# Five written instruction orders of a graph network's third layer, rewritten

## The chip, the cores and the metric

The kernel runs on one core of one Trainium2 chip. The metric is the device time of one execution in microseconds. The times shown are the median of three runs, with the lowest and highest, and beside them stands one more execution, which the hardware profiler recorded.

## The reference, cut to what matters

128 graphs of 64 nodes with 256 features pass through four layers. Each layer adds its result to its input and normalizes each node's 256 features.

```python
x = _layernorm(x + L0(x, adj, ...))   # five groups of 25 nodes, two graph convolutions each
x = _layernorm(x + L1(x, adj, W, b))  # one graph convolution
x = _layernorm(x + L2(x, adj, ...))   # a polynomial of the normalized adjacency, leaky relu
x = _layernorm(x + L3(x, adj, ...))   # five rounds of a gated recurrent unit:
# A = (adj != 0); h = x
# for l in range(5):
#     m = h @ weight[l];  agg = A^T m per graph
#     r, z = sigmoid(...); n = tanh(i_n + r * h_n);  h = (1 - z) * n + z * h
# x = _layernorm(x + h)
```

The reference numbers its layers from 0. All data are float32.

## The kernel before

The 128 graphs lie in 16 chunks of 8. Layer 0 comes first (up to about 320 us of the span). Layer 3 fills the rest, and layers 1 and 2 of the later chunks are done inside it.

**Steps of layer 3.** A step s (there are 79 in the loop) is one of the five rounds of one chunk. Two chunks alternate: step s works on chunk x, while w is the chunk of the step before, whose gates are being finished. Ten steps are a cycle: five rounds of an even chunk and five of an odd one, one after the other. Within a step the instructions stand in a written order, a string of names in `ORDERS` (L67). Sequence "p" serves steps 2 to 7 of a cycle; "8", "9", "0" and "1" serve the other four. `step` (L1138) walks through the string and issues what each name stands for. The loop runs under a manual schedule, so every engine (TensorE, VectorE, ScalarE, GpSimd and SyncE's DMA queue) executes its own share in exactly the order of the string. There is no planner at run time: an engine waits at the head of its queue until the data are there.

The names in the strings:

- R1 to R7 and N1 to N7: the seven products of a Strassen-like scheme on TensorE (L837), for the gates r and z together (eight 128x256 matmuls each) and for n (four each). Products 1, 6, 7 and 4 add into one PSUM bank a, in that order of use. Product 2 has bank b; 5 and 3 share bank d.
- r1, r6, r7 and n1, n6, n7: ScalarE copies the running content of bank a (L857), before the next product adds to it.
- A2, A7, A3 and B2, B7, B3: VectorE adds a copy to bank b or d (L861).
- S: two sigmoids on ScalarE (L938). X, x: the reset gate, two VectorE instructions (L995, L996). T, t: tanh (L953). U, u: the update, three VectorE instructions (L958 to L960). Capital letters belong to the step's own chunk, small ones to w. The digit (2, 7, 4 or 3) is the quarter of the state.
- f0, f1: VectorE transposes half of w's new state and SyncE writes it to DRAM (L974, L980). d0, d1: SyncE fetches it back, transposed (L988). G: the next round's messages: sixteen 128x128 matmuls on TensorE (L254), two ScalarE copies (L256), and three GpSimd sums Ta (L817 to L819).
- e, h: three GpSimd sums Th of the new state. y: two VectorE transposes and DMAs for the chunk that comes next. l: loads of the adjacency and x of a later chunk.
- p: one piece of other work: `output` of a finished chunk (L1074, four pieces), or else one piece of `mid` (L265), layers 1 and 2 of a coming chunk (19 pieces for each of two chunks in a cycle).

In `mid` the pieces that matter here are: the statistics of layer 1's result (L359), the pass that normalizes it (L362; four VectorE instructions of L185, one for each pair of graphs), the gather that multiplies the normalized rows with the polynomial (L366; TensorE again at L254, `pa<-poly,xt`), and at the end of layer 2 the statistics and the second normalizing pass (L381, L384). In the steady cycles, for the first chunk of a pair, L362 is the fifth p of step 3, L366 is the first p of step 4, and L384 is the first p of step 5. For the second chunk L362 is the fourth p of step 7, L366 the fifth p of step 7, and L384 the fifth p of step 8.

After the loop a short end runs the last round of the last chunk. It takes only the order of x, t and u from sequence "9" (L1211).

Of the kernel before, what the change touches and what calls it, by code (L numbers as in the profile page):

```python
# [41 lines left out]
class Unit:  # L42
# [23 lines left out]

ORDERS = {  # L67
    "p": """
u3 u4 R1 r1 t7 p R2 u7 l R5 h f0 f1 e R6 r6 d0 N1 A2 n1 N2 B2 p S2 N6 R7 X2 r7
n6 T2 p N5 R4 y A7 U2 N7 S7 n7 p S4 R3 B7 A3 N4 S3 X7 d1 N3 B3 X3 X4 G p T4 T3  # L70
""",
    "8": """
u4 l R1 R5 R2 t7 u3 f0 u7 e r1 R6 f1 N1 h p n1 p N2 d1 A2 r6 B2 N6 S2 d0 R7 N5
r7 X2 p n6 A7 R4 N7 p y n7 R3 B7 S4 S7 N4 A3 T2 X7 X4 N3 S3 B3 X3 U2 p T4 G T3
""",
    "9": """
u4 t7 l R1 R5 p R2 r1 u7 A2 u3 f0 h d0 R6 f1 p r6 p N1 d1 n1 N2 S2 B2 X2 R7 N6
r7 N5 n6 T2 N7 A7 U2 y R4 n7 R3 p S4 S7 e B7 N4 A3 S3 G N3 p X7 X4 B3 X3 p T4
T3
""",  # L80
    "0": """
l u4 t7 u3 R1 u7 R5 f0 R2 r1 R6 f1 N1 A2 h n1 r6 N2 S2 N6 R7 n6 B2 y N5 r7 p X2
N7 d0 T2 A7 n7 p B7 p e d1 U2 S7 R4 R3 A3 G S4 N4 p S3 N3 B3 X4 X3 T4 X7 T3
""",
    "1": """
u4 p t7 u3 f0 R1 R2 u7 R5 h l r1 f1 R6 r6 N1 N2 e n1 A2 N6 d0 R7 S2 B2 n6 r7 N5
p A7 N7 X2 n7 d1 T2 y p R4 B7 p R3 S7 A3 U2 S4 N3 B3 N4 S3 G X7 X3 X4 T4 T3 p
""",
}

# [1200 lines left out]
```

## Time and profile before

| what | value |
|---|---|
| median of three runs | 2134.34 us (2134.17 to 2135.53) |
| the profiled execution's own time | 2135.55 us |
| its span, first to last instruction | 2133.7 us |
| TensorE busy | 2109.1 us, 99% |
| VectorE busy | 1641.0 us, 77% |
| ScalarE busy | 979.1 us, 46% |
| GpSimd busy | 592.6 us, 28% |
| granted TensorE clock, mean | 0.997 |

"Busy" means that at least one instruction is in flight. TensorE's matmuls overlap, so a small wait between two of them can vanish in the busy share. In an undisturbed run of 128x256 matmuls one starts every 216 ns although each is recorded as 379 ns long; of 128x128 matmuls one starts every 111 ns. Waits are therefore best read from the starts. VectorE and GpSimd both work in SBUF, and how long a VectorE instruction takes here depends on what GpSimd does at the same time.

### The profile page before, as it was taken

What the parts mean: (1) busy time and instruction counts of PE and PEld (TensorE: products, weight loads), DVE (VectorE), ACT (ScalarE), POOL (GpSimd) and SP (SyncE); (2) the same over time, 40 slices, a digit from 0 to 9 for tenths busy, and PEclk for the clock granted to TensorE, in tenths of its full rate; (3) what the DMA queues carried; (4) which work ended last, traced back from release to release, by engine and by line L of the source; (5) the groups of instructions that cost most, each with busy time, mean ns of one, the idle gap of its engine ahead of it and who ended that gap; (6) DMA issues with size and microseconds to landing.
All of it is one profiled execution on the core that took longest, in us unless ns stands there. A gap on an engine that the chain in (4) does not pass through costs nothing.

```text
span 2133.7 us, 31438 instructions
## 1 busy us (share of the span) xinstructions
PE 2109.1 (99%) x10738; PEld 1819.5 (85%) x10738; DVE 1641.0 (77%) x3849; ACT 979.1 (46%) x2006; POOL 592.6 (28%) x638
## 2 busy tenths in 40 slices
PE   9999999999999999999999999999999999999997
PEld 6777788888888888888888888888888888888886
DVE  3345566787988798788878898879887987888776
ACT  3333334444544454444544454544444554445443
POOL 3411121222332233222323232223222232223321
PEclk9999999999999999999999999999999999999998
DMA  6642110223421342124322342124212421233221
GB/s 167 178 133 62 36 41 21 55 60 75 90 65 40 73 91 75 47 59 78 86 50 50 70 95 68 47 65 93 71 40 65 96 68 46 55 69 91 50 50 40
DMA packets 522059, 149.80 MB, mean 70 GB/s; under 512 B 488734, under 2 KB 516924, under 8 KB 521900
## 3 DMA queue, kind: packets, MB, share of 16 engines
q1 hardware_dynamic: 516996, 142.58, 27.7%
q0 software_dynamic: 2192, 4.80, 0.9%
q8 instruction: 85, 1.39, 0.3%
q10 hardware_dynamic: 2712, 0.42, 0.1%
q14 instruction: 74, 0.61, 0.1%
HBM read 82.70 MB, written 65.01 MB: 69 GB/s over the span
## 4 chain that ended last, share of the span: by engine, by line
PE 91%; DVE 6%; DMA 1%; issue 1%; POOL 0%; ACT 0%; SPq 0%; POOLq 0%; DVEq 0%; ACTq 0%
PE parz L837 24%; PE pdrz L837 12%; PE pan L837 12%; PE pa L254 9%; PE pbrz L837 6%; PE pdn L837 6%; PE pd L333 5%; PE ps L524 5%; PE ph L508 4%; PE pbn L837 3%; PE pa L492 1%; PE pp L314 1%; PE po L546 1%; DVE xt L185 1%; PE pf L644 1%; DVE NI L996 1%
## 5 line engine op out<-in xcount | busy, mean ns | idle before, releaser
L857 ACT COPY c<-parz 128x512 f32<-128x512 f32 x240 | 140.0, 583 | 369.8 <-PE parz L837 368.8
L837 PE MATMUL parz<-Th,WHH 128*128 128x256 f32 x960 | 289.0, 383 | 2.9 <-ACT c L857 2.9
L938 ACT ACTIVATE RZ<-RZ,brz 128x256 f32<-128x256 f32 x474 | 214.9, 503 | 166.8 <-DVE RZ L861 166.7
L817 POOL TENSOR_TENSOR Ta<-agg 128x512 f32<-128x512 f32 x80 | 102.7, 1284 | 660.0 <-ACT agg L256 660.0
L837 PE MATMUL parz<-Ta,V 128*128 128x256 f32 x960 | 286.0, 380 | 0.0
L837 PEld LDWEIGHTS parz<-Th,WHH 128*128 128x128 f32 x960 | 178.9, 190 | 35.6 <-ACT c L857 10.4
L837 PEld LDWEIGHTS parz<-Ta,V 128*128 128x128 f32 x960 | 182.5, 190 | 24.8
L953 ACT ACTIVATE NI<-NI,bih 128x256 f32<-128x256 f32 x316 | 152.6, 506 | 109.2 <-DVE NI L996 108.9
L857 ACT COPY c<-pan 128x512 f32<-128x512 f32 x237 | 138.4, 584 | 130.4 <-PE pan L837 130.2
L170 POOL TENSOR_TENSOR rs<-ve,mhalf 128x4 f32<-128x4 f32 (+2 forms) x65 | 66.7, 1027 | 393.3 <-DVE ve L163 340.8
L959 DVE TENSOR_TENSOR RZ<-RZ 128x256 f32<-128x256 f32 x316 | 161.1, 510 | 10.8
L817 POOL TENSOR_TENSOR Th<-hn 128x512 f32<-128x512 f32 x64 | 81.5, 1274 | 293.1 <-DVE hn L960 281.3
L861 DVE TENSOR_TENSOR NI<-pdn,c 128x512 f32<-128x512 f32 x158 | 108.2, 685 | 59.9 <-ACT c L857 44.9
L861 DVE TENSOR_TENSOR RZ<-pdrz,c 128x512 f32<-128x512 f32 x160 | 109.7, 686 | 46.4 <-PE pdrz L837 25.3
L837 PE MATMUL pan<-Ta,V 128*128 128x256 f32 x474 | 145.4, 388 | 0.0
L995 DVE SCALAR_TENSOR_TENSOR NI<-NI,bhh,RZ 128x256 f32<-128x256 f32 x237 | 119.7, 505 | 30.2 <-ACT RZ L938 21.3
L837 PE MATMUL pan<-Th,WHH 128*128 128x256 f32 x474 | 141.0, 379 | 0.0
L958 DVE TENSOR_TENSOR RZ<-hn,NI 128x256 f32<-128x256 f32 x252 | 115.6, 459 | 27.8 <-ACT NI L953 27.2
L254 PEld LDWEIGHTS pa<-A,h 128*128 128x128 f32 x1024 | 124.4, 192 | 3.3
L254 PE MATMUL pa<-A,h 128*128 128x128 f32 x1024 | 124.6, 275 | 0.0
L256 ACT COPY agg<-pa 128x512 f32<-128x512 f32 x160 | 92.9, 583 | 62.9 <-PE pa L254 62.4
L960 DVE TENSOR_TENSOR hn<-RZ,NI 128x256 f32<-128x256 f32 x256 | 113.7, 444 | 9.1
(228 smaller groups left out, 4739.7 us busy)
## 6 DMA issues: line engine op xcount, KB each, us to landing
hb<-flip SPq DMA_DIRECT2D x184, 256.0 KB
h<-hb SPq DMA_DIRECT2D x624, 64.0 KB
out_dram<-xt SPq DMA_DIRECT2D x30, 256.0 KB
hT<-hb SPq DMA_DIRECT2D x112, 64.0 KB
W<-in_w_dram SPq DMA_DIRECT2D x10, 512.0 KB
xt<-xb SPq DMA_DIRECT2D x32, 156.0 KB
xo<-in_x_dram SPq DMA_DIRECT2D x9, 512.0 KB
xb<-xo SPq DMA_DIRECT2D x9, 512.0 KB
```

Source lines behind the costliest of these rows:

```text
L254: nc.tensor.matmul(p[:, q * 128 : (q + 1) * 128], src(q, k), m[:, q, :], start=True, stop=True)
L333: nc.tensor.matmul(p[:, h, :], ag[:, k, q * 128 : (q + 1) * 128], W[:, k, :], start=k == 0, stop=k == 1)
L817: nc.gpsimd.tensor_sub(t[:, 0:2, :], a[:, :, H:], a[:, 0, :].rearrange("p (s n) -> p s n", s=2))
L837: nc.tensor.matmul(bank[:, g, :], w[:, q, i - 1, :], rhs, start=i in (1, 2, 5) and g == 0 and m == 0, stop=m == len(side) - 1, skip_group_ ...
L857: nc.scalar.copy(c, self.a)
L861: nc.vector.tensor_add(v, self.b if i == 2 else self.d, self.copies.pop({7: 7, 2: 1, 3: 6}[i]))
L938: nc.scalar.activation(v, self.g.a[:, q, :] if i == 4 else v, AF.Sigmoid, bias=brz[:, 2 * q + j : 2 * q + j + 1])
L953: nc.scalar.activation(n, n, AF.Tanh, bias=bih[:, 4 + j : 5 + j])
L958: nc.vector.tensor_sub(d, self.hT[:, j, f], n)
L959: nc.vector.tensor_mul(d, d, z)
L960: nc.vector.tensor_add(self.hn[:, j, f], d, n)
L995: nc.vector.scalar_tensor_tensor(n[:, j, f], h, bhh[:, 4 + j : 5 + j], r[:, j, f], op0=ALU.add, op1=ALU.mult)
```

## The change

All five strings are replaced; nothing else is touched. Each new string holds the same names, so the same instructions are issued. Sequence 8 has one p more and sequence 9 one fewer (those had nothing to issue in the steady cycles), and in the steady cycles every piece stays in its step.

```diff
     "p": """
-u3 u4 R1 r1 t7 p R2 u7 l R5 h f0 f1 e R6 r6 d0 N1 A2 n1 N2 B2 p S2 N6 R7 X2 r7
-n6 T2 p N5 R4 y A7 U2 N7 S7 n7 p S4 R3 B7 A3 N4 S3 X7 d1 N3 B3 X3 X4 G p T4 T3
+t7 h u4 R1 u3 p l R2 u7 R5 r1 f0 f1 R6 d0 N1 r6 N2 n1 A2 e S2 B2 p R7 X2 N6 r7
+n6 T2 p A7 N5 R4 N7 S7 U2 n7 S4 p R3 N4 B7 A3 N3 S3 X7 d1 X4 B3 G p X3 T4 T3 y
 """,
     "8": """
-u4 l R1 R5 R2 t7 u3 f0 u7 e r1 R6 f1 N1 h p n1 p N2 d1 A2 r6 B2 N6 S2 d0 R7 N5
-r7 X2 p n6 A7 R4 N7 p y n7 R3 B7 S4 S7 N4 A3 T2 X7 X4 N3 S3 B3 X3 U2 p T4 G T3
+u4 t7 u3 R1 R5 p l f0 p u7 f1 h R2 d0 r1 R6 N1 n1 d1 N2 N6 p A2 r6 n6 S2 B2 y
+e R7 X2 N5 r7 A7 R4 N7 p n7 B7 S4 R3 N4 p S7 A3 X4 N3 B3 X7 S3 G X3 T2 p T3 U2
+T4
 """,
     "9": """
-u4 t7 l R1 R5 p R2 r1 u7 A2 u3 f0 h d0 R6 f1 p r6 p N1 d1 n1 N2 S2 B2 X2 R7 N6
-r7 N5 n6 T2 N7 A7 U2 y R4 n7 R3 p S4 S7 e B7 N4 A3 S3 G N3 p X7 X4 B3 X3 p T4
-T3
+t7 h R1 u4 R5 u3 r1 R2 A2 p u7 f0 R6 r6 d0 f1 N1 n1 N2 S2 l R7 r7 N6 n6 N5 B2 X2
+N7 A7 p d1 T2 R4 R3 p U2 S7 n7 e S4 y A3 B7 N4 S3 G N3 p X7 B3 X3 X4 T3 T4 p
 """,
     "0": """
-l u4 t7 u3 R1 u7 R5 f0 R2 r1 R6 f1 N1 A2 h n1 r6 N2 S2 N6 R7 n6 B2 y N5 r7 p X2
-N7 d0 T2 A7 n7 p B7 p e d1 U2 S7 R4 R3 A3 G S4 N4 p S3 N3 B3 X4 X3 T4 X7 T3
+t7 u4 h u3 u7 R1 R5 R2 r1 R6 f0 r6 f1 e N1 n1 A2 S2 N2 R7 N6 r7 n6 l B2 p N5 X2
+A7 N7 T2 d0 n7 R4 d1 p R3 B7 p S7 G S4 p A3 U2 N3 N4 B3 S3 X4 y X3 T3 X7 T4
 """,
     "1": """
-u4 p t7 u3 f0 R1 R2 u7 R5 h l r1 f1 R6 r6 N1 N2 e n1 A2 N6 d0 R7 S2 B2 n6 r7 N5
-p A7 N7 X2 n7 d1 T2 y p R4 B7 p R3 S7 A3 U2 S4 N3 B3 N4 S3 G X7 X3 X4 T4 T3 p
+p t7 R1 u7 u4 f0 u3 d0 R2 r1 R5 e A2 f1 R6 N1 n1 N2 r6 N6 n6 B2 p R7 S2 N5 r7 h
+l N7 n7 X2 y A7 T2 R4 R3 d1 p B7 p A3 U2 S7 N4 N3 S4 S3 B3 X4 G X3 T4 X7 T3 p
 """,
```

Read engine by engine, most names keep their neighbours. What moves is this:

- TensorE, sequence p: R7 and N6 change places. Sequence 8: the two products of layer 2 (p, p) stand before R2 instead of after N1. Sequence 0: R7 and N6 as well as N3 and N4 change places; sequence 1: N3 and N4. Sequence 9: no change.
- VectorE, sequence p: X4 moves ahead of B3, and X3 moves from ahead of the fifth p to behind it; u3 and u4 change places. Sequence 8: the second normalizing pass moves from the end (behind X3 and U2) to a place between B7 and A3; y moves ahead of X2; X7 moves behind B3. Sequences 9, 0 and 1: updates and gates change places among themselves; in sequence 1 X2 goes ahead of A7.
- ScalarE, sequence p: r1 moves from ahead of t7 to behind the first p; S2 moves ahead of the second p and S4 ahead of the fourth. Sequence 8: r1 stands behind the four evictions of the two products.
- GpSimd: the same order. SyncE: d0 before d1 in sequence 8; y's DMAs earlier in sequence 8; in sequence 1, d0's fetches stand ahead of f1's write; in sequence 0, the first output's stores stand behind d1.

## Prediction

> **What bounds the kernel now.** I read the page first: its busy line and the chain that ended last.
>
> ```profile
> span 2133.7 us, 31438 instructions
> ...
> PE 2109.1 (99%) x10738; PEld 1819.5 (85%) x10738; DVE 1641.0 (77%) x3849; ACT 979.1 (46%) x2006; POOL 592.6 (28%) x638
> ...
> PE 91%; DVE 6%; DMA 1%; issue 1%; POOL 0%; ACT 0%; SPq 0%; POOLq 0%; DVEq 0%; ACTq 0%
> ```
>
> TensorE carries the chain, and no edit removes a matmul. A new order can only win what TensorE waits. The busy share hides that, since overlapped matmuls look busy while they wait. So I read the starts in the timeline: 216 ns is the undisturbed step of a 128x256 matmul, 111 ns of a 128x128. The excess over these, summed over the starts, is 4.36 us in a steady cycle of ten steps (227.4 us; mean of the six cycles from step 10 to 69). By step: 0: 0.33, 1: 0.09, 2: 0.16, 3: 0.07, **4: 1.99**, 5: 0.61, 6: 0.09, 7: 0.16, 8: 0.33, 9: 0.52. The first ten steps wait 2.1 us together, the last nine of the loop 2.0. All of layer 3's loop therefore holds about 26 + 4 = 30 us, or 1.4%, and no order can give more.
>
> Who ends these waits, from the waits view (us in total, times, longest):
>
> ```profile
> PEld pa L254 <- DVE xt L185: 11.2, 18, 0.8
> PE pa L254 <- DVE xt L185: 6.4, 18, 0.4
> PEld pan L837 <- ACT c L857: 10.7, 46, 0.3
> PEld parz L837 <- ACT c L857: 10.4, 40, 0.9
> PEld pdrz L837 <- DVE RZ L861: 4.6, 12, 0.6
> ```
>
> The first two lines are one place, 3 matmuls in each of 6 cycles: the gather at the start of step 4 waits for the pass of L362. The timeline of one such place (start, length, instruction):
>
> ```profile
> 1318.42 0.68 DVE L861 TENSOR_TENSOR NI<-pdn,c 128x512 f32<-128x512 f32 x1
> 1319.20 0.48 DVE L995 SCALAR_TENSOR_TENSOR NI<-NI,bhh,RZ 128x256 f32<-128x256 f32 x1
> ...
> 1320.58 0.42 DVE L996 TENSOR_TENSOR NI<-pan,NI 128x256 f32<-128x256 f32 x1
> 1320.76 1.27 POOL L817 TENSOR_TENSOR Ta<-agg 128x512 f32<-128x512 f32 x1 [3.21 <-ACT agg L256]
> ...
> 1320.92 3.19 DVE L185 TENSOR_SCALAR xt<-xt,mv,rs 128x256 f32<-128x256 f32 x4
> ...
> 1322.23 0.49 PE L254 MATMUL pa<-poly,xt 128*128 128x128 f32 x2 [0.45 <-DVE xt L185]
> ...
> 1323.04 0.49 PE L254 MATMUL pa<-poly,xt 128*128 128x128 f32 x2 [0.32 <-DVE xt L185]
> ...
> 1323.84 1.70 PE L254 MATMUL pa<-poly,xt 128*128 128x128 f32 x12 [0.32 <-DVE xt L185]
> ```
>
> The pass starts 0.16 us after GpSimd's sums Ta (2.9 us for three), and each of its instructions ends just after one of the sums. Its four take 3.19 us; outside sums, in step 37, four take 1.37. The gather's first matmul was due at 1321.62 (R1 at 1319.89 plus eight times 0.216).
>
> **What the Trainium skill says.** "SBUF — State Buffer", section "Who interferes with whom": VectorE and GpSimd share one port pair, taken as an exclusive lock for a whole instruction; tensor_scalar in a two-port mode and any VectorE instruction with two SBUF inputs contend, one with an input in PSUM does not. The trace agrees: L185 406 ns free, 880 to 1256 under a sum; L959 425 against 990 on average; L861, which reads PSUM, 685 against 676. The pages put no price on the waits of this change; all durations below are the trace's.
>
> **The change part by part.** No instruction is added or removed. GpSimd's order is the same, so the sums stay where their inputs put them. On SyncE the loads l stay ahead of f0, and in sequence 0 an output's two stores go behind d1's fetches: nobody waits for a store.
>
> (a) *First pass, sequence p.* In step 43 VectorE had A3 to 1317.65, X7 to 1318.50, B3, X3, X4 to 1321.00, the pass to 1324.11. In the new order X4 follows X7: its product N4 ends at 1317.41 and its sigmoid S4 at 1316.24, so it runs 1318.42 to 1319.35; B3 (N3 ends 1318.27) to 1319.95; the pass starts at 1319.9, one microsecond earlier. One starts every 0.32 us, so three are through or in flight when Ta comes at 1320.76, and the fourth waits for one sum (1.28) and ends near 1322.35. The gather reads it at 1321.62 + 6 x 0.111 = 1322.29. The wait shrinks from 1.98 to about 0.2 us (0 to 0.8): **-1.78 a cycle**.
>
> (b) *What goes under the sum instead.* X3 (0.93 us, both inputs in SBUF) follows the pass. Under the sums I estimate it at 1.3 to 1.9. T3 waits for X3; behind T3 on ScalarE stand t7 and now r1 (0.5 + 0.5 + 0.6 us), and R6 waits for r1. Laid out from the trace: after step 3, X3 ends near 1323.9, r1 near 1326.5 (behind the gather's two copies), R6 is due at 1326.86: covered by 0.3. After steps 2, 5 and 6 the cover is 0.6, 0.7 and 2 us. After step 4 there is no TensorE piece between R1 and R6: statistics to 1349.3, X3 to 1350.2-1351.3, r1 to 1351.9-1352.95, R6 due at 1352.21. I take 0.3 (0 to 0.75). Step 5's waits at R3 and N3 (0.44) come from a late VectorE, which now starts u4 0.3 earlier; I keep 0.1. Net -0.04.
>
> (c) *R7 ahead of N6.* N6 waits for n1, copied while only N2 runs (0.08 in steps 2 and 5, 0.06 in 6); R7 fills that gap. R4 waited for r7 behind N5 alone (0.08 in 5 and 7); now N6 stands between too. R7's own copy r6 ends at R6 + 0.7, with N1 and N2 (1.73) as cover. **-0.38**.
>
> (d) *Sequence 8.* R7's wait of 0.24 for r6 goes (r6 ends 0.4 before R7). But r1 now stands behind four evictions of layer 2's products and ends at about R6's due time: +0.2; N6 behind N2 alone: +0.08. The second pass runs off the sums (1.4 us instead of 1.8) but waits for its GpSimd root, about 1.1 us after the statistics; behind it A3, S3 and X3, whose product N3 ends later anyway. y comes 5.7 us earlier: its two transposes (0.69 each) fill VectorE's wait for the sigmoid S2 ahead of X2, and its ten DMAs stand on SyncE behind d0 and d1 as before, with nothing of this step after them: free. Net +0.03.
>
> (e) *Sequences 9, 0, 1.* VectorE leaves step 8 about 1.4 us earlier, so R3's wait in 9 goes: -0.11; R5's 0.26 for Ta stays, its order is the same. In 0, N6's 0.13 goes, but T4 and t7 come later behind X3, X4: R6 and R3 +0.2; net +0.07. In 1, A7 now waits for X2 (0.93), and ends where R3 is due: +0.2 (0 to 0.5). In 1, d0's fetches precede f1's write, but f0's write lands (2.57 us) before f1 is transposed: free, with 1.4 us to spare before G; if that cover goes, G waits by what is missing.
>
> Sum: -1.78 - 0.04 - 0.38 + 0.03 - 0.11 + 0.07 + 0.2 = **-2.0 a cycle**, -12.1 in six. First ten steps: -0.6 by (c). Last nine: no pieces, (c) alone, six times 0.16: -1.0. The end, where R6 waits 2.3 us for a copy behind T3: T3 comes earlier, the updates not; I take -1 (-3.8 to +2, unknown). Together **-14.7 us**. Against the profiled execution's own 2135.55 (span 2133.7 and 1.85 around it) that is 2120.9; the median of the runs shown lies 1.2 lower, so **2119.6**.
>
> VectorE doesn't become the bound: 190.3 us busy in a cycle of 227.4.
>
> **Rivals.** *The likeliest (0.76)*, as above. Its own range is 2112 (no residual waits, the end at its best) to 2129.
>
> *The pass stays under the sum (0.10).* If S4 or N4 holds X4 up, or the sums take the lock before the second instruction of the pass, (a) falls to about -0.2: -14.7 + 6 x 1.6 = -5, so 2129 to 2131. For it: only 0.86 us separate pass and sum. Against: both of X4's inputs are ready a microsecond before.
>
> *Slower: the gate X3 takes the pass's place under the sum (0.11).* In all steps 2 to 7 of a cycle r1 now hangs on X3, T3 and t7. It decides when R6 waits more than 14.7/36 = 0.41 us a step on average. At 0.7 us, which needs X3 some 1.0 us later than I lay it out in most steps, the cost is 36 x 0.7 = 25, the net +10.5, and the time 2145. Against: four of the six places have 0.6 us of cover or more.
>
> *Small mishaps cancel the gain (0.03)*: 2134.
>
> **How the numbers follow.** This kernel's runs can tell about 0.2%, 4.3 us, from no change. Faster by more: the likeliest case, and half of the one where the pass stays under: 0.80. Within: 0.09. Slower: the gate case: 0.11. The range 2111 to 2134 holds the likeliest and the pass rival with their bounds and leaves the slower one out.
>
> **What would show it.** In step 4 the gather's matmuls follow R1 at 111 ns with at most the fourth pair late, and L185's mean in xt falls from 521 ns; the two lines of L254 on L185 in the waits shrink to under 3 us. Steps 2 to 7 lose their 0.08s at N6 and R4. New lines, if I am wrong: parz on c L857 growing beyond 10 us with R6 of steps 3 to 8 as the waiter, and pdrz on RZ L861 in step 1. A steady cycle above 227 us refutes the sum.

## The result and the profile after

| | before | after |
|---|---|---|
| median of six runs each | 2134.82 us (2133.23 to 2135.56) | 2124.94 us (2124.42 to 2125.68) |
| profiled execution: span | 2133.7 us | 2123.7 us |
| TensorE busy | 2109.1 us | 2102.9 us |
| VectorE busy | 1641.0 us | 1661.1 us |

The changed kernel takes 0.9954 of the time before (95% interval 0.9943 to 0.9964): 9.9 us less. The forecast of 2119.6 us is 5.3 us too low; its sum was -14.7.

The page after, busy line and chain:

```profile
span 2123.7 us, 31527 instructions
...
PE 2102.9 (99%) x10738; PEld 1820.6 (86%) x10738; DVE 1661.1 (78%) x3849; ACT 978.9 (46%) x2006; POOL 594.8 (28%) x638
...
PE 86%; DVE 10%; issue 1%; DMA 1%; ACT 0%; SPq 0%; POOL 0%; DVEq 0%; POOLq 0%; ACTq 0%
```

TensorE still carries the chain. VectorE is busy 20 us longer with the same 3849 instructions: something else now lies beside GpSimd's sums.

Where the 9.9 us lie, from the starts of R1 in both traces: first ten steps 223.59 to 223.00 us, the six cycles 1365.95 to 1359.23, steps 70 to 77 of the last nine 160.93 to 159.88, the rest from step 78 on 57.30 to 55.78. That is -0.6, **-6.7**, -1.05 and -1.5; the prediction had -0.6, **-12.1**, -1.0 and -1. Almost the whole error lies in the steady cycles.

There, the excess of the starts of TensorE's matmuls over their undisturbed steps, in us for a cycle, by step (the measure of the prediction; in all kernels against the undisturbed steps of the kernel before):

| step | 0 | 1 | 2 | 3 | 4 | 5 | 6 | 7 | 8 | 9 | sum |
|---|---|---|---|---|---|---|---|---|---|---|---|
| before | 0.33 | 0.09 | 0.16 | 0.07 | 1.99 | 0.61 | 0.09 | 0.16 | 0.33 | 0.52 | 4.36 |
| after | 0.44 | 0.41 | 0.53 | 0.07 | 0.09 | 0.79 | 0.09 | 0.08 | 0.47 | 0.28 | 3.24 |
| predicted change | +0.07 | +0.2 | -0.08 | 0 | -1.78 | -0.20 | -0.06 | -0.08 | +0.03 | -0.11 | -2.0 |
| measured change | +0.11 | +0.32 | +0.37 | 0 | -1.90 | +0.18 | 0 | -0.08 | +0.14 | -0.24 | -1.1 |

Step 4 did what was said. In the waits view of after (total us, times, longest) the two lines of L254 on L185 are gone; the waits for the copies c (r and n) became fewer, and the longest of them longer:

```profile
PEld parz L837 <- ACT c L857: 12.5, 27, 1.9
PEld pan L837 <- ACT c L857: 8.3, 31, 0.6
```

The timeline of after at the place that the prediction showed of before, step 43 into 44:

```profile
1316.94 2.32 DVE L185 TENSOR_SCALAR xt<-xt,mv,rs 128x256 f32<-128x256 f32 x4
...
1317.82 1.29 POOL L817 TENSOR_TENSOR Ta<-agg 128x512 f32<-128x512 f32 x1 [3.20 <-ACT agg L256]
...
1318.69 2.02 PE L254 MATMUL pa<-poly,xt 128*128 128x128 f32 x16
1319.19 1.01 DVE L995 SCALAR_TENSOR_TENSOR NI<-NI,bhh,RZ 128x256 f32<-128x256 f32 x1
...
1320.23 0.83 DVE L996 TENSOR_TENSOR NI<-NI 128x256 f32<-128x256 f32 x1
...
1322.86 0.59 ACT L857 COPY c<-parz 128x512 f32<-128x512 f32 x1
...
1324.00 0.38 PE L837 MATMUL parz<-Th,WHH 128*128 128x256 f32 x1
```

The pass now starts 0.88 us ahead of the sum instead of 0.16 us behind it and takes 2.32 us instead of 3.19, and the sixteen matmuls of the gather go through with no idle time noted. X3 (L995, L996) lies under the sums instead, and takes 1.87 us instead of 0.93. Its copy r1 ends at 1323.45, and R6 at 1324.00 doesn't wait for it.

Two new waits answer for most of the missing gain; a third, in step 21 alone, comes under (e) below. **Step 2**, here step 42 of after, where X7 is the last gate of the new sequence 1:

```profile
1270.42 1.56 DVE L995 SCALAR_TENSOR_TENSOR NI<-NI,bhh,RZ 128x256 f32<-128x256 f32 x1
1270.43 1.27 POOL L817 TENSOR_TENSOR Ta<-agg 128x512 f32<-128x512 f32 x1 [3.73 <-ACT agg L256]
...
1272.01 0.83 DVE L996 TENSOR_TENSOR NI<-NI 128x256 f32<-128x256 f32 x1
...
1272.77 0.94 DVE L290 TENSOR_TENSOR dg<-eyec,rsum 128x256 f32<-128x256 f32 x1
...
1273.75 0.51 ACT L294 ACTIVATE poly<-dg,cw 128x256 f32<-128x256 f32 x1 [2.59 <-DVE dg L290]
...
1274.16 0.49 ACT L953 ACTIVATE NI<-NI,bih 128x256 f32<-128x256 f32 x1
...
1274.56 0.57 ACT L857 COPY c<-parz 128x512 f32<-128x512 f32 x1
...
1275.17 0.30 PEld L837 LDWEIGHTS parz<-Th,WHH 128*128 128x128 f32 x2 [0.67 <-ACT c L857]
```

In before the last gate of this place is X4, which reads PSUM (`pan`) and isn't stretched, though it lies under the sum (1273.82 to 1275.09):

```profile
1273.81 0.48 DVE L995 SCALAR_TENSOR_TENSOR NI<-pan,bhh,RZ 128x256 f32<-128x256 f32 x1
```

X7 takes 2.42 us under the sum instead of about 0.9; behind it on VectorE stands dg, an instruction of layers 1 and 2's piece; ScalarE's activation of that piece (L294) waits for dg and stands ahead of t7 and r1; and R6 waits for r1. That is 0.54 us in step 2 of five of the six cycles and nothing in step 22, which follows the long wait of step 21: 0.45 us a cycle on average.

**Step 5**, here the change from step 44 to 45 of after:

```profile
1345.39 0.79 POOL L819 TENSOR_TENSOR Ta<-agg,Ta 128x256 f32<-128x256 f32 x1
...
1345.52 0.95 DVE L958 TENSOR_TENSOR RZ<-hn,NI 128x256 f32<-128x256 f32 x1
...
1352.32 0.65 DVE L861 TENSOR_TENSOR RZ<-pbrz,c 128x512 f32<-128x512 f32 x1
...
1353.01 0.91 ACT L938 ACTIVATE RZ<-RZ,brz 128x256 f32<-128x256 f32 x2 [2.26 <-DVE RZ L861]
...
1353.82 0.56 ACT L857 COPY c<-parz 128x512 f32<-128x512 f32 x1
...
1354.43 0.30 PEld L837 LDWEIGHTS parz<-Th,WHH 128*128 128x128 f32 x2 [0.40 <-ACT c L857]
```

The same instruction in before, step 45, which starts as the last sum ends:

```profile
1350.72 0.41 DVE L958 TENSOR_TENSOR RZ<-hn,NI 128x256 f32<-128x256 f32 x1
```

The updates do start earlier against R1 (3.34 us behind it instead of 3.69), as predicted. But so they come under the last sum: the first update's first instruction (L958) takes 0.95 us instead of 0.41, and the lead is gone. A2 starts 10.14 us behind R1 instead of 9.96, S2 and then r7 follow it on ScalarE, and R4's wait for r7 grows from 0.08 to 0.26 us, by the same 0.18.

### The profile page after: what moved, and what is told of

Read it like the earlier page. It is cut to its first block, busy times and chain, and to the rows that moved or that the text cites. A ratio compares the mean times of both kernels' runs of the same rounds, so it can differ in the third digit from the quotient of the medians.

```text
span 2123.7 us, 31527 instructions
## 1 busy us (share of the span) xinstructions
PE 2102.9 (99%) x10738; PEld 1820.6 (86%) x10738; DVE 1661.1 (78%) x3849; ACT 978.9 (46%) x2006; POOL 594.8 (28%) x638
## 4 chain that ended last, share of the span: by engine, by line
PE 86%; DVE 10%; issue 1%; DMA 1%; ACT 0%; SPq 0%; POOL 0%; DVEq 0%; POOLq 0%; ACTq 0%
PE parz L837 22%; PE pdrz L837 12%; PE pan L837 11%; PE pa L254 8%; PE pdn L837 5%; PE pbrz L837 5%; PE pd L333 5%; PE ps L524 5%; PE ph L508 4%; PE pbn L837 3%; DVE NI L995 1%; PE pa L492 1%; PE pp L314 1%; DVE NI L996 1%; PE po L546 1%
## 5 line engine op out<-in xcount | busy, mean ns | idle before, releaser
L817 POOL TENSOR_TENSOR Ta<-agg 128x512 f32<-128x512 f32 x80 | 103.7, 1296 | 662.4 <-ACT agg L256 662.3
L837 PEld LDWEIGHTS parz<-Th,WHH 128*128 128x128 f32 x960 | 179.5, 190 | 35.5 <-ACT c L857 12.5
L817 POOL TENSOR_TENSOR Th<-hn 128x512 f32<-128x512 f32 x64 | 81.6, 1275 | 315.2 <-DVE hn L960 304.4
L958 DVE TENSOR_TENSOR RZ<-hn,NI 128x256 f32<-128x256 f32 x252 | 133.9, 532 | 34.8 <-ACT NI L953 34.4
L959 DVE TENSOR_TENSOR RZ<-RZ 128x256 f32<-128x256 f32 x316 | 150.9, 478 | 10.7
L861 DVE TENSOR_TENSOR NI<-pdn,c 128x512 f32<-128x512 f32 x158 | 108.1, 684 | 58.8 <-ACT c L857 55.3
L996 DVE TENSOR_TENSOR NI<-NI 128x256 f32<-128x256 f32 x237 | 137.9, 582 | 8.2
L861 DVE TENSOR_TENSOR RZ<-pdrz,c 128x512 f32<-128x512 f32 x160 | 109.6, 685 | 37.3 <-PE pdrz L837 26.0
L995 DVE SCALAR_TENSOR_TENSOR NI<-NI,bhh,RZ 128x256 f32<-128x256 f32 x237 | 129.1, 545 | 6.3 <-ACT RZ L938 1.4
L254 PEld LDWEIGHTS pa<-A,h 128*128 128x128 f32 x1024 | 124.5, 192 | 4.8 <-issue 1.5
L254 PE MATMUL pa<-A,h 128*128 128x128 f32 x1024 | 124.9, 275 | 1.4 <-DMA h<-hb 1.4
```

Of the source, the lines that this page charges most:

```text
L254: nc.tensor.matmul(p[:, q * 128 : (q + 1) * 128], src(q, k), m[:, q, :], start=True, stop=True)
L817: nc.gpsimd.tensor_sub(t[:, 0:2, :], a[:, :, H:], a[:, 0, :].rearrange("p (s n) -> p s n", s=2))
L837: nc.tensor.matmul(bank[:, g, :], w[:, q, i - 1, :], rhs, start=i in (1, 2, 5) and g == 0 and m == 0, stop=m == len(side) - 1, skip_group_ ...
L861: nc.vector.tensor_add(v, self.b if i == 2 else self.d, self.copies.pop({7: 7, 2: 1, 3: 6}[i]))
L958: nc.vector.tensor_sub(d, self.hT[:, j, f], n)
L959: nc.vector.tensor_mul(d, d, z)
```

## The experiments

Ratios are to runs of the kernel before on the same chip. The experiments ran on several chips, whose medians of the kernel before lie between 2134.5 and 2135.3 us, so differences between two runs of under about 1 us say little.

**e1: only the gate behind the pass.** The kernel before with two moves in p:

```diff
-n6 T2 p N5 R4 y A7 U2 N7 S7 n7 p S4 R3 B7 A3 N4 S3 X7 d1 N3 B3 X3 X4 G p T4 T3
+n6 T2 p N5 R4 y A7 U2 N7 S7 n7 p S4 R3 B7 A3 N4 S3 X7 d1 N3 X4 B3 G p X3 T4 T3
```

> The kernel before with one edit in sequence p: X4 ahead of B3, and X3 behind the fifth p. If the pass of L362 running under GpSimd's sum is what TensorE waited for (lock theory), the gather's wait in step 4 falls from 1.98 to 0.2 us or less in each of six cycles, some of it given back by X3 under the sum: 8 to 11.5 us faster than before. If the gain of the change came from its other moves (rest theory), this edit brings 0 to 2 us.

Measured: 2126.04 us (2125.33 to 2127.15), 0.9959 (0.9947 to 0.9972), so 8.8 us less. The gather's wait falls from 1.98 to 0.08 us; step 5 rises from 0.61 to 0.94, with R4 at 0.34. This pair of moves carries most of the gain, and brings the loss in step 5 with it.

**e2: only the gate put back.** The changed kernel with X3 and X4 ahead of the pass again:

```diff
-n6 T2 p A7 N5 R4 N7 S7 U2 n7 S4 p R3 N4 B7 A3 N3 S3 X7 d1 X4 B3 G p X3 T4 T3 y
+n6 T2 p A7 N5 R4 N7 S7 U2 n7 S4 p R3 N4 B7 A3 N3 S3 X7 d1 B3 X3 X4 G p T4 T3 y
```

> The changed kernel with X3 (and B3 ahead of it, X4 behind it) put back ahead of the fifth p. Lock theory: the gather in step 4 waits about 2 us again and the time goes back up by 8 to 11 us, to 2133 to 2136. Rest theory: up by no more than 2 us, to 2125 to 2127.

Measured: 2135.86 us (2134.71 to 2136.78), 1.0005 (0.9997 to 1.0013): 10.9 us above the changed kernel. The gather waits 1.98 us again, and step 5 is at 0.61 again, as in the kernel before. Without this move the other edits, taken together, win nothing that can be measured; the loss of sequence 1 (e6) is among them.

**e3: only R7 ahead of N6.** The kernel before with one exchange in p:

```diff
-u3 u4 R1 r1 t7 p R2 u7 l R5 h f0 f1 e R6 r6 d0 N1 A2 n1 N2 B2 p S2 N6 R7 X2 r7
+u3 u4 R1 r1 t7 p R2 u7 l R5 h f0 f1 e R6 r6 d0 N1 A2 n1 N2 B2 p S2 R7 N6 X2 r7
```

> The kernel before with R7 ahead of N6 in sequence p and nothing else. By the prediction's part (c) the waits of 0.06 to 0.08 us at N6 and R4 go in steps 2, 5, 6, 7 and in the last nine steps: 3.5 us faster (2 to 4.5). Rival: such waits only move on to the next product, and the time changes by less than 1 us.

Measured: 2132.35 us (2131.25 to 2133.93), 0.9987 (0.9981 to 0.9994), so 2.5 us less. The first ten steps win 0.57 us and the last nine 1.1, as laid out. In the cycles only 0.12 of the 0.38 us a cycle arrive (starts of R1: 1365.95 to 1365.22 us for six): 0.08 goes in steps 2 and 7 each, but in step 6 the 0.06 us passes from N6 to R7, in step 5 R3 takes over what N6 leaves (0.25 to 0.32), and steps 0 and 9 grow by 0.03 each.

**e4: only sequence p new.** The strings 8, 9, 0 and 1 are those of the kernel before:

```diff
-u3 u4 R1 r1 t7 p R2 u7 l R5 h f0 f1 e R6 r6 d0 N1 A2 n1 N2 B2 p S2 N6 R7 X2 r7
-n6 T2 p N5 R4 y A7 U2 N7 S7 n7 p S4 R3 B7 A3 N4 S3 X7 d1 N3 B3 X3 X4 G p T4 T3
+t7 h u4 R1 u3 p l R2 u7 R5 r1 f0 f1 R6 d0 N1 r6 N2 n1 A2 e S2 B2 p R7 X2 N6 r7
+n6 T2 p A7 N5 R4 N7 S7 U2 n7 S4 p R3 N4 B7 A3 N3 S3 X7 d1 X4 B3 G p X3 T4 T3 y
```

> The new sequence p with the old sequences 8, 9, 0 and 1. By the waits read in the changed kernel, steps 2 to 7 hold the whole gain (1.4 us a cycle, 10 us in all) and the other four sequences lost 0.3 us a cycle: so 10 to 12 us faster than before, at or a little below the changed kernel. Rival: the other sequences brought half of it, and this kernel is only 5 us faster than before.

Measured: 2121.40 us (2121.01 to 2123.14), 0.9937 (0.9924 to 0.9951): 13.5 us less than before, more than the 10 to 12 us expected, and 3.5 us less than the kernel with all five new strings. Step 2 shows 0.08 us and no wait at R6. So the other four strings together cost time.

**e5: r1 ahead of t7.** The changed kernel with one move in p:

```diff
-t7 h u4 R1 u3 p l R2 u7 R5 r1 f0 f1 R6 d0 N1 r6 N2 n1 A2 e S2 B2 p R7 X2 N6 r7
+h u4 R1 r1 t7 u3 p l R2 u7 R5 f0 f1 R6 d0 N1 r6 N2 n1 A2 e S2 B2 p R7 X2 N6 r7
```

> The changed kernel (2123 to 2125 us) with one edit: in sequence p the copy r1 stands ahead of t7 and u3 instead of behind R5. It is for step 2, where R6 waits 0.45 us a cycle in the changed kernel because r1 stands on ScalarE behind one of M3's activations and then t7. Theory 1 (the wait is ScalarE's order): r1 comes about 0.57 us earlier, R6's wait falls from 0.45 to about 0.1 in step 2 and nothing else moves, so -0.3 to -0.4 us a cycle and about -2 us against the changed kernel. Theory 2 (R6 waits because X7 and T3 are late, whatever stands between): r1 still waits behind T3 and the activation, R6's wait stays above 0.35, and the time is within 0.5 us of the changed kernel's.

Measured: 2122.94 us (2121.86 to 2123.9), 0.9944 (0.9932 to 0.9957): 2.0 us below the changed kernel. R6's wait in step 2 falls from 0.45 to 0.09. X7 is still the last gate under the sum, and r1 still stands behind the activation L294; with t7 behind r1 most of the wait goes. So the wait takes both, X7 at the end of sequence 1 (which e6 undoes) and t7 ahead of r1 in p.

**e6: the old sequence 1.** The changed kernel with this string put back:

```diff
-p t7 R1 u7 u4 f0 u3 d0 R2 r1 R5 e A2 f1 R6 N1 n1 N2 r6 N6 n6 B2 p R7 S2 N5 r7 h
-l N7 n7 X2 y A7 T2 R4 R3 d1 p B7 p A3 U2 S7 N4 N3 S4 S3 B3 X4 G X3 T4 X7 T3 p
+u4 p t7 u3 f0 R1 R2 u7 R5 h l r1 f1 R6 r6 N1 N2 e n1 A2 N6 d0 R7 S2 B2 n6 r7 N5
+p A7 N7 X2 n7 d1 T2 y p R4 B7 p R3 S7 A3 U2 S4 N3 B3 N4 S3 G X7 X3 X4 T4 T3 p
```

> The changed kernel with the old string of sequence 1 alone put back (p, 8, 9 and 0 stay new). Theory 1 (of the 3.5 us that the four other new sequences cost, most lies in sequence 1, whose last gate is X7 under GpSimd's sum): step 2's wait at R6 goes from 0.45 to below 0.1, step 1's waits at G and N6 (0.3 to 0.4 a cycle) go too, together 0.6 to 0.8 us a cycle, so 2.5 to 4.5 us less than the changed kernel. Theory 2 (the cost lies in sequences 8 and 0, at r1 behind layer 2's evictions and at A7 behind X2): at most 1 us less than the changed kernel, and step 2's wait at R6 stays.

Measured: 2120.34 us (2120.2 to 2121.05), 0.9934 (0.992 to 0.9947): 4.6 us below the changed kernel. Step 1 falls from 0.41 to 0.12, step 2 from 0.53 to 0.10. It lies 1.1 us below e4 too (0.7 when each is taken against the kernel before on its own chip), so the new strings 8, 9 and 0 cost nothing together and win a little, above all in the end (55.8 us instead of 57.3). The loss goes with sequence 1.

**e7: an extra sum under the pass.** The changed kernel, with an operation that only GpSimd does and nobody reads:

```diff
+                if s % (2 * L) == 3:
+                    t = work.tile([128, 2, H], F32, name="extra", bufs=1)
+                    nc.gpsimd.tensor_sub(t, x.NI[:, :, 0, H:], x.NI[:, :, 0, H:])
```

> The changed kernel with one operation more: in step 3 of every cycle GpSimd subtracts two SBUF tiles of 128x512 elements into a scratch tile that nobody reads, ahead of G's sums, so that it runs while VectorE does the pass of L362 (eight such subtractions in all, none on TensorE or VectorE). Theory 1 (GpSimd's operation holds the pass up instruction by instruction): L185's instructions in step 3 stretch again from 0.4 to 0.9 to 1.3 us, Ta itself comes up to 1.3 us later, and the gather of step 4 waits 0.7 to 2 us a cycle again: +5 to +9 us against the changed kernel. Theory 2 (the pass was late in the kernel before, by where it was started, and what GpSimd does beside it costs little): 0 to +1 us, and the gather's wait stays below 0.3 us.

Measured: 2133.73 us (2132.7 to 2134.27), 0.9995 (0.9987 to 1.0003): 8.8 us above the changed kernel, nearly the whole gain. The timeline of e7 in step 43, and the line of L254 in its view by source (us, times):

```profile
1321.14 3.52 DVE L185 TENSOR_SCALAR xt<-xt,mv,rs 128x256 f32<-128x256 f32 x4
```
```profile
1321.30 1.14 POOL L1172 TENSOR_TENSOR extra<-NI 128x512 f32<-128x512 f32 x1 [2.48 <-DVE NI L861]
...
1322.40 1.31 POOL L817 TENSOR_TENSOR Ta<-agg 128x512 f32<-128x512 f32 x1
```
```profile
  DVE xt L185: 11.1, 24
```

The order on VectorE is the changed kernel's, the pass starts at the same place (0.02 us ahead of step 4's R1 in both), and it still takes 3.52 us instead of 2.32, since a GpSimd operation comes 0.16 us behind its start, as Ta did in the kernel before. The gather waits 1.27 us a cycle instead of 0.08. It is what GpSimd does beside the pass that holds it up, not the place of the pass as such.

**e8: the second pass on ScalarE.** The kernel of e4 with r1 ahead of t7 in p (as in e5), in the old sequence 8 r6 directly behind N1 and n1 behind it (ahead of both p), and the pass of L384 moved for the even chunk:

```diff
-        norm_apply(xt, *norm)
+        if first or c % 2:
+            norm_apply(xt, *norm)
+        else:
+            nb = small.tile([128, NP], F32, name="nb")
+            nc.vector.scalar_tensor_tensor(nb, norm[0][:, :, 0], -1.0, norm[1], op0=ALU.mult, op1=ALU.mult)
+            norm_apply(xt, norm[0], norm[1], nb, "a")
```

> The kernel with only sequence p new (2121.4 us) plus three edits: r1 ahead of t7 in p; in the old sequence 8, r6 directly behind N1; and the second normalizing pass of the even chunk (L384, first p of step 5) as four ScalarE activations with scale and bias instead of four VectorE instructions (1.4 us). Theory 1 (step 5's waits at R3, R4 and N3, 0.79 us a cycle, come from a VectorE queue that is late from the pass on): step 5's waits fall to 0.1 to 0.4, step 8's wait at R7 (0.24) goes, together 0.6 to 0.9 us a cycle, so 4 to 6 us less than the kernel with p alone, about 2116. Theory 2 (these waits are ScalarE's: r7 and S2 queue there, and four activations more make that worse): step 5's waits stay or grow, and the time is between 2120 and 2124.

Measured: 2119.72 us (2118.39 to 2120.58), 0.9929 (0.9917 to 0.9942): 1.7 us below e4, less than the first theory had (about 2116). R3, R4 and N3 of step 5 wait no more, so VectorE's late queue was their cause; step 8 falls from 0.34 to 0.09. But step 5 still loses 0.64 us, now at R7 (timeline of e8, step 45; the lines of this kernel stand 6 higher, L863 is the copy):

```profile
1343.67 2.07 ACT L183 ACTIVATE xt<-xt,nb,rs 128x256 f32<-128x256 f32 x4 [1.73 <-DVE nb L389]
...
1345.65 0.56 ACT L863 COPY c<-parz 128x512 f32<-128x512 f32 x1
...
1346.26 0.30 PEld L843 LDWEIGHTS parz<-Th,WHH 128*128 128x128 f32 x2 [0.76 <-ACT c L863]
```

r6 stands behind the four activations: one wait was exchanged for another.

**e9 and e10: the pass split.** e8 with `"av"` in place of `"a"` (pairs 0 and 2 on ScalarE, 1 and 3 on VectorE) and the new sequence 9, run twice.

> The kernel of the run before (sequence p new with r1 ahead of t7, old 8 with r6 directly behind N1, old 0 and 1; 2119.7 us) with two edits: the second normalizing pass of the even chunk is split, pairs 0 and 2 on ScalarE and pairs 1 and 3 on VectorE, and sequence 9 is the changed kernel's. Theory 1: the 0.62 us a cycle that step 5 now waits at R7 come from r6 standing on ScalarE behind four activations (2.1 us); with two of them r6 is a microsecond earlier and R7 doesn't wait, VectorE is 0.7 us later but has that much room, so step 5 falls from 0.64 to 0.0 to 0.2 us; step 9 falls from 0.55 to the 0.28 that the new string showed. Together -0.7 to -0.9 us a cycle and 4 to 6 us in all, about 2115. Theory 2 (VectorE has no room): the waits at R3, R4 and N3 come back to 0.4 us or more, and the time is between 2118 and 2121.

> The same kernel as the run before, once more: its five times there fell into two groups, 2116.1 and 2116.7 against 2120.7 to 2121.1, and its profile was of the lower group. If the two groups belong to the kernel, they come back here, at about 2116.5 and 2121; if a profile of the upper group is caught, it should show the 4.5 us in one place of the run, not spread over the cycles. If they don't belong to it, all times are near 2116 or near 2121.

Measured: 2120.73 us (2116.08 to 2121.11), 0.9929 (0.9915 to 0.9942), and 2117.68 us (2115.99 to 2120.16), 0.9916 (0.9902 to 0.993). The ten times are spread from 2116.0 to 2121.1, not in two groups. e9's median lies in the second theory's range, but not for its reason: step 5 falls to 0.22 us in both traces (R7 at 0, N3 at 0.20), so VectorE had the room; step 9 stays at 0.5, so its smaller sum in the changed kernel doesn't come from the new string 9. The traces, of executions at 2116.08 and 2120.16 us, differ in two places: step 40 (its sum is 1.4 us in one, nearly all at R3, and 4.6 in the other, at R6) and the end (56.0 against 57.3). In step 39 of the slower one:

```profile
1222.77 1.27 POOL L822 TENSOR_TENSOR Ta<-agg 128x512 f32<-128x512 f32 x1 [12.14 <-ACT agg L256]
```
```profile
1223.08 2.98 DVE L1086 SCALAR_TENSOR_TENSOR xt<-h,mask,xt 128x128 f32<-128x128 f32 x4 [1.99 <-DMA h<-hb]
```

A fetch lands 2 us later, `output`'s four instructions so come under the sum and take 2.98 us instead of 1.12, and everything behind them on VectorE, with t7 and r1 behind that, is late by both. Of the 4.6 us, 2.9 are R6's wait for r1; the rest is the clock, which the trace has at half (0.50) for the next 3.41 us, while R6 runs (see the last section). R6 of step 40 waits 0.7 to 0.9 us in before, e3 and e4 too, but in none of the six traces with the new sequence 0. Why the fetch is late in some executions stays open.

**e11: a version that beats both.** The changed kernel with the old sequence 1 (as e6), r1 ahead of t7 (as e5), the split pass (as e9), and in sequence 8

```diff
-u4 t7 u3 R1 R5 p l f0 p u7 f1 h R2 d0 r1 R6 N1 n1 d1 N2 N6 p A2 r6 n6 S2 B2 y
+u4 t7 u3 R1 R5 r1 p l f0 p u7 f1 h R2 d0 R6 N1 n1 d1 N2 N6 p A2 r6 n6 S2 B2 y
```

> The changed kernel with the old sequence 1 (2120.3 us in an earlier run) and three edits: r1 ahead of t7 in sequence p, r1 directly behind R5 in sequence 8 (ahead of the evictions of layer 2's two products), and the second normalizing pass of the even chunk split between ScalarE (pairs 0, 2) and VectorE (pairs 1, 3). Theory 1 (each remaining wait has the one cause named for it): step 5 falls from 0.80 to 0.3 or less, as the split pass did in the run before, and step 8 from 0.47 to 0.2, where R6's 0.24 goes; -0.7 to -0.8 us a cycle, 4 to 5 us in all, so 2115 to 2116.5. Theory 2 (the evictions of sequence 8 are then late and its VectorE adds with them, or the split pass has no room in this arrangement): step 8 or step 5 keeps its sum, and the time is 2118 to 2121.

Measured: 2114.88 us (2114.3 to 2115.59), 0.9906 (0.9892 to 0.992): 20.4 us below the kernel before on the same chip, and 10.1 below the median of the changed kernel. Step 5 is at 0.23 and step 8 at 0.17; the sum of a cycle is 1.44 us, against 4.36 before and 3.24 after. The line of parz in the waits view, of e6 and then of e11:

```profile
PEld parz L837 <- ACT c L857: 9.2, 22, 1.9
```
```profile
PEld parz L842 <- ACT c L862: 4.2, 10, 1.9
```

## Why the prediction was right or wrong

The gain came from where it was expected, the gather of step 4, but 9.9 of the 14.7 us arrived, since small terms of the sum were misjudged. Of the signs named ahead, L185's mean in xt fell from 521 to 451 ns and the two lines of L254 went; parz on c did grow beyond 10 us (12.5), with R6 as the waiter, though in steps 2 and 8.

**(a), the first pass: right.** -1.78 predicted, -1.90 measured. e1 and e2 show that the place of X3 and X4 against the pass decides it, e7 that GpSimd's operation is the cause. The rival in which the pass stays under the sum is out. The Trainium skill's page "SBUF — State Buffer", section "Who interferes with whom", on which the step rested, agrees with e7.

**(b), X3 under the sum: half right.** X3 took 1.87 us, inside the 1.3 to 1.9 laid out, and R6 of step 5 waits for nothing; in no step 3 to 7 did r1 come late, so the slower rival is out for sequence p. The sum had R3 and N3 of step 5 fall from 0.44 to 0.1 because u4 starts earlier. u4 did, by 0.35 us, but nothing was said of what runs on GpSimd at that earlier time: L958 also has two SBUF inputs, and took 0.95 us under the last sum. R3 and N3 are at 0.52 together, R4's grew, and the step as a whole was put at -0.20 and was +0.18.

**(c), R7 ahead of N6: right at both ends, mis-sized in the cycles.** e3 puts 1.7 of its 2.5 us outside of them. In the steady cycles the term of -0.38 is -0.12 in e3: a wait of 0.06 to 0.08 us taken away at one product came back at the next one in steps 5 and 6.

**(d), sequence 8.** R6's +0.2 behind the evictions (0.24) and N6's +0.08 (0.08) came as said, R7's 0.24 went; R4's 0.05 more was missed. **(e), sequences 9 and 0** were right in sign (-0.24 for -0.11, +0.11 for +0.07), in part by luck. In 9, R3's 0.11 went as said, but R5's wait, which was to stay at 0.26, fell to 0.13 as well, in every trace with the new sequence 8 and in no other. In 0, R6 and R3 were to wait 0.2 more; R6 waits for nothing, and N7, which nobody named, waits 0.18.

**(e), sequence 1: the step that failed.** The sum put +0.2 there, for A7 behind X2. That wait (R3) didn't come. The step missed what stands behind X7, now the last gate, in the next step: 0.45 us a cycle at R6 of step 2. (b) laid out the cover of R6 behind steps 2 to 6, and nobody laid it out behind step 1, where the activation of layers 1 and 2's piece stands ahead of t7. It is the slower rival's mechanism, but in one step of the cycle and not in six.

A further 1.6 us are a wait of the messages G for a fetch in step 21 alone. (e) called it free to put d0's fetches ahead of f1's write, since f0's write lands before f1 is transposed, with 1.4 us to spare. The two do fall together (10.2 and 10.1 us behind R1), but then SyncE issues the four fetches for 1.8 us before it comes to f1's write, which so goes out 12.1 us behind R1 instead of 9.8, and d1's first fetch starts at 14.8 us instead of 12.7 in a usual cycle (steps 41 of after and before). In step 21 of after f1's write is slow to land, and the fetch waits 4.1 us for it where 2.2 is usual (waits of SyncE's queue in that step: total, times, longest):

```profile
SPq L988 <- DMA hb<-flip: 6.2, 2, 4.1
```

The fetch is 1.9 us later and G waits 1.6, so about 0.3 us were left of the cover. Of the steps 1 of all cycles, only step 21 has G wait for more than 0.1 us, and it does in all four traces with the new sequence 1 (after, e2, e5, e7: 1.6, 1.4, 1.1 and 1.2 us), and in none with the old one. Why the write is slow in this step was not settled. e6 gives the whole step: 4.6 us where 1.2 (six times 0.2) were counted.

So the parts are: p alone -13.5 (e4), where (a) to (c) had -14.8 with the first and the last steps; sequence 1 +4.6 (e6), where +1.2 was counted; sequences 8, 9 and 0 with the end -1.1 (e6 against e4), where -1.1 was counted. That these add up to the measured -9.9 proves nothing, since the three differences lead from before to after by way of e4 and e6; but they place the missing 4.8 us: 1.3 in p and 3.4 in sequence 1. A small misreading beside it: 227.4 us is the length of one steady cycle of before, the mean of the six is 227.7.

**The end** was put at -1 and is -1.5, close by luck: the waits hardly shrink. In the kernel before R6 waits 2.2 us in one piece there, and the clock falls; in the changed one two waits of 0.5 and 1.5 us stand 8 us apart, and it doesn't. Windows of before and of after (us; busy time of five engines with instructions; then granted TensorE clock, DMA share and GB/s):

```profile
2101.70:2105.70 4.00, 3.25 (x11) 2.78 (x12) 2.59 (x6) 1.84 (x6) 0.00 (x0) 0.77 0.01 2
2105.70:2109.70 4.00, 4.00 (x18) 3.34 (x17) 0.00 (x0) 0.67 (x3) 0.72 (x1) 0.81 0.00 0
```
```profile
2091.70:2095.70 4.00, 4.00 (x20) 3.54 (x19) 4.00 (x10) 0.00 (x0) 1.12 (x2) 1.00 0.00 0
```

The 0.77 and 0.81 are means: the view of before gives 0.50 for the stretch from 2103.83 to 2107.25 us, and 1.00 for as long before and behind it. The traces of e1, e3, e4, e8 and e10, with the old or nearly old sequence 8, show the low clock too (57.3 us from step 78 to the end), and all with the new one 55.8. e9 and e10, one program without the fall and with it, differ by 1.3 us there, so the fall makes up most of the 1.5.

## What to carry to other kernels

Before an instruction is moved to an earlier time, list what another engine that shares its memory ports does at that time, and also for the instructions behind it, which move along: here the moved pass, the gate that took its place and the update after the gate were three tenants of one sum. Put under such a sum what doesn't mind it (here the gates that read PSUM, the PSUM adds, the statistics and the transposes), and last the operation with the most cover behind it. A string that is good by itself must be read across its seam to the next one: the loss of sequence 1 lay in the step that follows it, and waits of under 0.1 us that an edit seems to remove can come back one product later (in e3, 0.12 of 0.38 us a cycle were won).

## What the runs showed of the hardware

The stretching goes by the inputs. In after, the mean duration of VectorE's instructions that overlap one of the sums of L817 to L819, against that of the others (worked out from the trace), is: L996 from SBUF 935 against 424 ns, but L996 with `pan` in PSUM 424 against 424; L995 680 against 478, with `pan` 477 against 476; L958 929 against 416; L185 846 against 408. The statistics L160, with one input, take 396 against 401, the transposes L974 689 against 694, and the PSUM adds L861 671 against 684.

The clock fell after a wait of only 2.2 us. The Trainium skill's page "TensorE: Matmul & The Clock Gate", section "Part 1: The HAM clock gate (the "warmup" mystery)", has the half clock after an idle window of about 3.4 us, and windows that run freely. The traces agree with the half clock and the length of the window (0.50 for 3.41 us), but no window had to be idle as a whole. In before the clock falls at 2103.83 us and next falls 20.48 us later, six times 3.41. Counted in windows of 3.41 us that end where the clock falls, TensorE was idle (from the recorded end of a matmul to the start of the next) in the window ahead of the fall for 2.0 us in before, 2.1 in e8, 2.2 in e1, e3, e4 and e10, and 2.4 in step 40 of e10.

That also sorts e9 from e10, which are the same program: both wait 2.2 us at the same place in the end, but e9's clock stays at 1.00 and its end takes 56.0 us instead of 57.3. Counted back from the next fall in e9's trace (2107.56 us, seven windows), a border at 2083.67 us cuts its wait into 1.6 and 0.6 us. In after the longer of the two waits gives 1.5 us in a window. So in these traces 2.0 us of idle time in one window were enough (in the last windows of the span, 1.9) and 1.6 were not. That the windows decide is read from where the falls lie, and was not tried by moving a wait.
